# Four graph-attention layers on one core: the next batches' nodes loaded by SP instead of GpSimd, and the input test spread over layer 3 instead of layer 2

## The chip, the cores and the metric

The kernel runs on one core of a Trainium2 chip. The time is that of one execution on the device, in microseconds. I quote medians of several executions and, for comparisons, the ratio of means with its 95% interval. All executions quoted here were in the fast state; a run's profile comes from one execution of it. The profiled execution of the kernel before took 3149.0 us, 8 us less than the median of the others, so a difference between its trace and another's comes out some us smaller than that between medians. The granted TensorE clock is given as a share of full speed.

Names of the engines in the profile: PE is TensorE's matmuls, PEld its weight loads, DVE is VectorE, ACT is ScalarE, POOL is GpSimd, SP is SyncE. L409 is a line of the kernel; later kernels are a few lines shorter or longer, so the same statement has a neighbouring number.

## The reference, cut to what matters

Sixteen graphs of 1024 nodes with 256 features pass four layers of graph attention, each behind a layer norm:

```
# layer 0 (layers 1 and 2 alike with another activation; layer 3 has 4 heads)
h = maximum(layernorm(x), 0)
x = x + attention(h, adj)          # softmax over masked scores, then scores @ (h @ W)
```

`adj` is int32, 16 x 1024 x 1024. The fast path of the kernel is right only if its entries are 0 or 1, so the kernel also tests that, and falls back to a slow general path if the test fails.

## The kernel before

Two streams of batches, the even and the odd ones, run side by side, half a batch apart; a generator yields estimated times and decides whose code is traced next. The build then orders each engine's instructions itself: it may draw an instruction forward into an earlier gap, unless `keep_in_program_order` pins it behind the last instruction traced on the same engine. An engine takes its list in order, as the trace below shows for VectorE: from 455.2 us it stands idle for 2.22 us at reductions whose nodes have not landed, though the matmuls that feed the `inv` behind them end at 456.0 us.

```python
nodes = tile_pool("nodes", bufs=3)          # x_b: three buffers; adjs: four
...
def fetch_nodes(b):
    xs[b] = nodes.tile([P, NI, D], F32, name="x_b")
    queue = nc.gpsimd if b > 1 else nc.sync
    fetch = queue.dma_start(xs[b]..., in_blocks(x[b]))        # 1 MB
    if b > 0:
        tc.keep_in_program_order(fetch)

def load(b):                     # traced by batch b-2, step by step
    for c in range(4):
        ... nc.gpsimd.dma_start(rows[c], adj[b, ...])         # int32 to bytes, to DRAM; pinned
    if b < 2:
        fetch_nodes(b)
    yield
    mask = masks[b] = nodes.tile(..., name="mask")
    for c in range(4):
        ... nc.sync.dma_start_transpose(mask[:, c], ...)      # the turning transfers; pinned
        yield
    if b > 1:
        fetch_nodes(b)
        yield

def test(b):
    for i in range(NI):          # 8
        adj_i = adjs.tile([P, N], BF, name="adj_i")
        fetch = nc.gpsimd.dma_start(adj_i, adj[b, rows i])    # pinned for batch 0 only
        square = nc.scalar.activation(adj_i, adj_i, AF.Square, ..., accum_out=squares[...])
        tc.keep_in_program_order(square)
        yield
...
def first(pair):                 # a batch begins: sums for the layer norm
    nc.vector.tensor_reduce(sums[:, pair], xb[:, pair, :], AX.X, ALU.add)
    yield from project(...)
...
# finishing of a layer, row block by row block
finish(i, acc, sums[:, i : i + 1])
if l == 2:
    next(testing)
...
# layer 3: eight pieces (four heads, two halves)
for n in range(H * NH):
    ... 8 matmuls into accT
    nc.scalar.copy(sums, accT)
    next(coming, None)           # one step of load(b + 2)
    ... TensorE turns sums; inv; y; per head: bias, relu, norm, rescale
```

Of the kernel before, what the change touches and what calls it, by code (L numbers as in the profile page):

```python
# [59 lines left out]
def short_path(ctx: ExitStack, tc: tile.TileContext, ins: dict, out: bass.AP, bad: bass.AP):  # L60

    nc = tc.nc
    x, adj = ins["x"], ins["adj"]
# [31 lines left out]
    def in_blocks(a: bass.AP) -> bass.AP:  # L95
        return a.rearrange("(c p t) f -> p c t f", p=P, t=2)

    xs, masks = {}, {}
    narrows = [dram.tile([N, N // 2], BF, name=f"narrow{n}") for n in range(2)]

    def fetch_nodes(b: int):
        xs[b] = nodes.tile([P, NI, D], F32, name="x_b")
        queue = nc.gpsimd if b > 1 else nc.sync
        fetch = queue.dma_start(xs[b].rearrange("p (c t) f -> p c t f", t=2), in_blocks(x[b]))
        if b > 0:
            tc.keep_in_program_order(fetch)

# [25 lines left out]
    def test(b: int):  # L133

        for i in range(NI):

            adj_i = adjs.tile([P, N], BF, name="adj_i")
            fetch = nc.gpsimd.dma_start(adj_i, adj[b, ts(i, P), :])  # L138
            if b == 0:
                tc.keep_in_program_order(fetch)  # L140


            square = nc.scalar.activation(  # L143
                adj_i, adj_i, AF.Square, bias=minus_half, accum_out=squares[:, b, i : i + 1]
            )
            tc.keep_in_program_order(square)
            yield
# [116 lines left out]
    def accumulator(b: int) -> bass.AP:  # L264
        return psum.tile([P, HALF], F32, name=f"acc{b % 2}")
# [40 lines left out]
    def weigh(b: int, column, c, op, into: list):  # L306


        while row_taken:
            yield 0.25  # L310
        row_taken.append(b)
        r = psum.tile([P, N], F32, name="row", bufs=1)
        for i in range(NI):
            nc.tensor.transpose(r[:, ts(i, P)], column(i).to_broadcast([P, P]), ident)  # L314
        yield 0.5
        for j in range(NI):
            w = edges.tile([P, N], F32, name=f"weights{b % 2}")
            nc.vector.scalar_tensor_tensor(w, r, c(j), masks[b][:, j // 2, :, j % 2], op0=op, op1=ALU.mult)  # L318
            into.append(w)
            if j == NI - 1:  # L320
                row_taken.pop()
            yield 0.5

    def start(behind, b: int):

        for t in behind:
            if row_taken == [b]:
                return
            yield t
# [19 lines left out]
    def batch(b: int):  # L349
# [4 lines left out]
        testing = test(b)  # L354

        def begin(l: int):

            V = nodes.tile([P, NI, H, E + 1], F32, name="V", bufs=4).rearrange("p i h e -> p i (h e)")

            def evict(i: int, projected: bass.AP, rstd: bass.AP):  # L360
                nc.scalar.activation(V[:, i, D : D + 3], projected[:, D:], AF.Exp, scale=rstd)  # L361
                if l == 2:
                    nc.scalar.mul(V[:, i, :D], projected[:, :D], rstd)
                else:
                    nc.vector.tensor_scalar(  # L365
                        V[:, i, :D], projected[:, :D], rstd, V[:, i, D : D + 1],
                        op0=ALU.mult, op1=ALU.mult,
                    )

            return V, evict  # L370
# [4 lines left out]
        def begin3():  # L375
            h3 = last["h3"] = single.tile([P, NI, D], F32, name="h3")
            V3 = nodes.tile([P, NI, H, E + 1], F32, name="V", bufs=4)
            ex = last["ex"] = small.tile([P, NI, 3 * H], F32, name="ex", bufs=2)

            def evict3(i: int, projected: bass.AP, rstd: bass.AP):  # L380
                nc.scalar.activation(ex[:, i, :], projected[:, D:], AF.Exp, scale=rstd)
                nc.scalar.mul(h3[:, i, :], projected[:, :D], rstd)
                q = ex[:, i, :H].unsqueeze(2)
                nc.gpsimd.tensor_mul(
                    V3[:, i, :, :E], h3[:, i, :].rearrange("p (h e) -> p h e", h=H),
                    q.to_broadcast([P, H, E]),
                )
                nc.gpsimd.tensor_copy(V3[:, i, :, E:], q)
                nc.gpsimd.tensor_add(xb[:, i, :], xb[:, i, :], beta)

            return V3, evict3

        def attend(l: int, V: bass.AP, finish, then: int):

            weights = []
            behind = weigh(
                b, lambda i: V[:, i, D + 2 : D + 3], lambda j: V[:, j, D + 1 : D + 2],
                ALU.min if l == 1 else ALU.max, weights,
            )
            yield from start(behind, b)  # L400
            following = begin(then) if then < 3 else begin3()
            steps = iter(())
            accs = {}
            sums = small.tile([P, NI], F32, name="sums_of_x")

            def product(i: int, j: int):
                if j == 0:
                    accs[i] = accumulator(b)[:, : D + 1]
                nc.tensor.matmul(  # L409
                    accs[i], weights[j][:, ts(i, P)], V[:, j, : D + 1],  # L410
                    start=(j == 0), stop=(j == NI - 1),
                )


            for j in range(NI):
                next(behind)
                product(0, j)
                product(1, j)
                if b == 0 and j == NI - 1:


                    next(preparing)
                    if l == 0:
                        next(loading[1])
                    next(preparing, None)
                yield 0.9
            for _ in behind:
                pass
            for i in range(NI):
                if i > 1:  # L430
                    for j in range(NI):
                        product(i, j)
                acc = accs.pop(i)
                finish(i, acc, sums[:, i : i + 1])
                if l == 2:
                    next(testing)
                if i != 0:
                    yield 3.6
                if i % 2 == 1:

                    yield from steps
                    steps = project(b, then, xb, sums, i // 2, following[1])
                yield from islice(steps, 1)
            yield 1.0
            yield from steps
            return following[0]
# [9 lines left out]
        def finish(i: int, acc: bass.AP, total: bass.AP):  # L456
            add_elu(xb[:, i, :], acc, total)
# [50 lines left out]
        def weigh3(h: int):  # L508
            if h == H:
                return iter(())  # L510
            return weigh(
                b, lambda i: ex[:, i, 2 * H + h : 2 * H + h + 1],
                lambda j: ex[:, j, H + h : H + h + 1], ALU.max, weights,
            )
# [3 lines left out]
        for n in range(H * NH):  # L518
            h, g = divmod(n, NH)
            if g == NH - 1:  # L520

                behind = weigh3(h + 1)
                yield from start(behind, b)

            accT = accumulator(b)[: E + 1, :]
            for j in range(NI):
                if n == 0:
                    next(behind)
                nc.tensor.matmul(  # L529
                    accT, V3[:, j, h, :], weights[h * NI + j][:, ts(g, HALF)],  # L530
                    start=(j == 0), stop=(j == NI - 1),
                )
                if n > 0:
                    next(behind, None)
                yield 0.9
            for _ in behind:
                pass
            sums = wide.tile([E + 1, HALF], F32, name="sums")
            nc.scalar.copy(sums, accT)
            next(coming, None)  # L540
            yield 0.5
            acc = psum.tile([P, NG, E + 1], F32, name="misc")
            for i in range(NG):
                nc.tensor.transpose(acc[:, i, :], sums[:, ts(i, P)], ident[: E + 1, : E + 1])  # L544
            inv = small.tile([P, NG], F32, name="inv4")
            inverse(inv, acc[:, :, E])
            nc.vector.tensor_mul(  # L547
                y[:, ts(g, NG), h, :], acc[:, :, :E], inv.unsqueeze(2).to_broadcast([P, NG, E])
            )
            yield 0.5  # L550
            if g == NH - 1:
                if h > 0:
                    rescale(*normed.pop())
                normed.append(center(h))
                yield 1.0
# [21 lines left out]
    while streams:  # L577
        ahead = min(streams, key=lambda s: s[0])
        t = next(ahead[1], None)
# [381 lines left out]
```

## Time and profile before

| | before |
|---|---|
| time, median | 3157.41 us (3155.65 to 3158.07) |
| span of the profiled execution | 3147.4 us |
| TensorE busy | 2992.1 us, 95% |
| VectorE, ScalarE, GpSimd busy | 67%, 35%, 31% |
| node loads on GpSimd | 14, of 1 MB, 5.6 us from issue to landing |
| VectorE idle until nodes land | 68.6 us, 15 times; 6.0 us of it at the program's first load, which SP issues |

The prediction below shows the lines and reads them. TensorE's busy share looks full, but a stall can cost twice here: idle time, and a slower clock just after it (in the stretch 450 to 470 us below, 16.09 of 20 us busy and a mean clock of 0.91).

### The profile page before, as it was taken

The numbers are of one execution on the slowest core, as the hardware profiler recorded it, in microseconds if no ns is written. First come the engines' busy times: TensorE is split into PE (matmuls) and PEld (weight loads), VectorE is DVE, ScalarE is ACT, GpSimd is POOL, SyncE is SP. The second block draws the span as 40 slices with busy tenths as digits, with TensorE's granted clock in tenths as the row PEclk, the third lists the DMA queues.
The fourth block names the chain that finished last, engine by engine and source line by source line (L and its number), as shares of the span: only waits on it lengthen the run. The fifth ranks groups of instructions, "written<-read, shape, count | busy, mean of one in ns | idle before, by whom it ended". The sixth has DMA issues, their size and how long they took to land.

```text
span 3147.4 us, 36526 instructions
## 1 busy us (share of the span) xinstructions
PE 2992.1 (95%) x12678; PEld 2054.9 (65%) x12678; DVE 2122.3 (67%) x4595; ACT 1095.7 (35%) x3009; POOL 966.2 (31%) x1469
## 2 busy tenths in 40 slices
PE   7999999999999999999999999999999999999986
PEld 6776756657576675766757667575665757657652
DVE  5666677665867667676676776667766676766755
ACT  2433424234242342524324243342423424234240
POOL 2222323233242332323233232332322324233233
PEclk9999999999999999999999999999999999999998
DMA  7212212112122112212122120221211212002010
GB/s 122 37 23 38 41 27 44 18 34 41 27 47 21 41 27 41 38 17 51 18 41 41 16 52 14 41 41 27 44 18 33 41 27 48 7 14 41 1 27 15
DMA packets 116880, 105.59 MB, mean 34 GB/s; under 512 B 73680, under 2 KB 91216, under 8 KB 116688
## 3 DMA queue, kind: packets, MB, share of 16 engines
q0 software_dynamic: 44256, 81.80, 16.1%
q1 hardware_dynamic: 72432, 21.37, 3.4%
q8 instruction: 103, 1.69, 0.2%
q14 instruction: 89, 0.73, 0.1%
HBM read 153.49 MB, written 33.55 MB: 59 GB/s over the span
## 4 chain that ended last, share of the span: by engine, by line
PE 67%; DVE 20%; POOL 4%; ACT 3%; DMA 3%; issue 2%; SPq 0%; DVEq 0%; ACTq 0%; POOLq 0%
PE acc L409 32%; PE acc L529 19%; PE acc L297 11%; DVE weights L318 10%; PE misc L290 2%; DMA x_b<-in_x_dram 2%; PE row L314 2%; POOL rstd L261 2%; POOL y L489 1%; DVE x_b L345 1%; DVE x_b L344 1%; DVE sums_of_x L463 1%; DVE V L365 1%; DVE centered L274 1%; PE misc L544 1%
## 5 line engine op out<-in xcount | busy, mean ns | idle before, releaser
L409 PE MATMUL acc<-V,weights 128*128 128x257 f32 x6144 | 1446.0, 383 | 43.4 <-DVE weights L318 32.6
L409 PEld LDWEIGHTS acc<-V,weights 128*128 128x128 f32 x6144 | 1145.0, 190 | 362.4 <-DVE weights L318 107.4
L529 PE MATMUL acc<-weights,V 128*65 128x512 f32 x2048 | 965.6, 597 | 1.9 <-DVE weights L318 1.5
L318 DVE SCALAR_TENSOR_TENSOR weights<-row,ex,mask 128x1024 f32<-128x1024 f32 x512 | 630.2, 1275 | 19.6 <-PE row L314 10.6
L297 PE MATMUL acc<-W,hT 128*128 128x259 f32 (+1 forms) x2048 | 516.7, 390 | 28.3 <-ACT hT L292 12.6
L529 PEld LDWEIGHTS acc<-weights,V 128*65 128x65 f32 x2048 | 275.3, 139 | 362.5 <-issue 317.6
L318 DVE SCALAR_TENSOR_TENSOR weights<-row,V,mask 128x1024 f32<-128x1024 f32 x384 | 478.7, 1276 | 45.9 <-PE row L314 45.9
L297 PEld LDWEIGHTS acc<-W,hT 128*128 128x128 f32 x2048 | 377.7, 191 | 145.1 <-ACT hT L292 39.2
L341 ACT ACTIVATE below<-acc,inv 128x256 f32<-128x256 f32 x256 | 121.2, 473 | 751.2 <-DVE inv L334 610.2
L281 ACT ACTIVATE square<-x_b,minus_mean 128x256 bf16<-128x256 f32 x512 | 260.4, 509 | 306.5 <-DVE minus_mean L271 297.8
L261 POOL TENSOR_TENSOR rstd<-rstd,minus_half 128x2 f32<-128x2 f32 (+1 forms) x320 | 298.1, 932 | 21.1
L489 POOL TENSOR_TENSOR y<-y,bias 128x512 f32<-128x512 f32 x64 | 81.7, 1276 | 668.1 <-DVE y L547 637.9
L260 POOL TENSOR_SCALAR rstd<-squared 128x2 f32<-128x2 f32 x256 | 64.7, 253 | 639.7 <-ACT square L281 639.0
L292 ACT ACTIVATE hT<-misc 128x512 f32<-128x512 f32 x256 | 149.6, 597 | 211.7 <-PE misc L290 210.3
L274 DVE TENSOR_SCALAR centered<-x_b,minus_mean 128x256 f32<-128x256 f32 x512 | 167.0, 371 | 52.8 <-PE misc L290 48.9
L344 DVE SCALAR_TENSOR_TENSOR x_b<-below,x_b 128x256 f32<-128x256 f32 x256 | 123.0, 481 | 100.4 <-ACT below L341 99.9
L290 PEld LDWEIGHTS misc<-ident,centered 128*128 128x128 f32 x1024 | 126.6, 143 | 88.4 <-issue 50.8
L361 ACT ACTIVATE V<-acc,rstd 128x3 f32<-128x3 f32 x384 | 97.8, 260 | 242.0 <-PE acc L297 241.3
L138 POOL DMA_DIRECT2D adj_i<-in_adj_dram x128 | 76.6, 599 | 338.9 <-ACT adj_i L143 185.5
L333 DVE TENSOR_SCALAR inv<-acc 128x1 f32<-128x1 f32 x256 | 38.6, 154 | 209.6 <-PE acc L409 208.2
L290 PE MATMUL misc<-ident,centered 128*128 128x128 f32 x1024 | 155.8, 278 | 19.0 <-DVE centered L274 18.8
L365 DVE TENSOR_SCALAR V<-acc,rstd,V 128x256 f32<-128x256 f32 x256 | 133.9, 539 | 57.6 <-ACT V L361 56.8
(74 smaller groups left out, 2165.3 us busy)
## 6 DMA issues: line engine op xcount, KB each, us to landing
adj_i<-in_adj_dram POOLq DMA_DIRECT2D x128, 256.0 KB, 3.9
narrow<-in_adj_dram POOLq DMA_DIRECT2D x64, 256.0 KB, 9.4
out_dram<-y POOLq DMA_DIRECT2D x32, 512.0 KB, 4.0
x_b<-in_x_dram POOLq DMA_DIRECT2D x14, 1024.0 KB, 5.6
x_b<-in_x_dram SPq DMA_DIRECT2D x2, 1024.0 KB, 7.4
mask<-narrow SPq DMA_TRANSPOSE x64, 3.7
W<-in_L_gnn_W_dram SPq DMA_DIRECT2D x3, 256.0 KB, 6.4
weights<-in_L_gnn_a_dram SPq DMA_DIRECT2D x3, 256.0 KB, 8.1
```

The lines of the kernel that those rows point to most:

```text
L261: nc.gpsimd.tensor_tensor(r, r, minus_half.to_broadcast([P, n]), op=ALU.pow)
L274: nc.vector.tensor_scalar(centered[:, n, :], xb[:, 2 * pair + n, :], minus_mean[:, n : n + 1], 0.0, op0=ALU.add, op1=ALU.max,)
L281: nc.scalar.activation(square, xb[:, 2 * pair + n, :], AF.Square, bias=minus_mean[:, n : n + 1], accum_out=squared[:, n : n + 1],)
L290: nc.tensor.transpose(turned[:, k, ts(n, P)], centered[:, n, ts(k, P)], ident)
L292: nc.scalar.mul(hT, turned, ROOT_D)
L297: nc.tensor.matmul(projected, hT[:, k, ts(n, P)], W[l][:, k, :], start=(k == 0), stop=(k == NK - 1),)
L318: nc.vector.scalar_tensor_tensor(w, r, c(j), masks[b][:, j // 2, :, j % 2], op0=op, op1=ALU.mult)
L341: nc.scalar.activation(below, acc[:, :D], AF.Exp, scale=inv)
L344: nc.vector.scalar_tensor_tensor(xi, below, 1.0, xi, op0=ALU.min, op1=ALU.add)
L365: nc.vector.tensor_scalar(V[:, i, :D], projected[:, :D], rstd, V[:, i, D : D + 1], op0=ALU.mult, op1=ALU.mult,)
L409: nc.tensor.matmul(accs[i], weights[j][:, ts(i, P)], V[:, j, : D + 1], start=(j == 0), stop=(j == NI - 1),)
L529: nc.tensor.matmul(accT, V3[:, j, h, :], weights[h * NI + j][:, ts(g, HALF)], start=(j == 0), stop=(j == NI - 1),)
```

## The change

The intent: take the loads of later nodes out of GpSimd's busy list and put them on SP, behind the turning transfers of the same batch; and take the test's row loads and squares out of layer 2, where ScalarE has an elu per row, into the eight pieces of layer 3. The whole diff:

```diff
@@ fetch_nodes
-        queue = nc.gpsimd if b > 1 else nc.sync
-        fetch = queue.dma_start(xs[b]..., in_blocks(x[b]))
+        fetch = nc.sync.dma_start(xs[b]..., in_blocks(x[b]))
@@ finishing of a layer
                 finish(i, acc, sums[:, i : i + 1])
-                if l == 2:
-                    next(testing)
@@ layer 3, each piece
             nc.scalar.copy(sums, accT)
+            next(testing)
             next(coming, None)
```

More of the change, by code (lines that the diff above doesn't have):

```diff
@@ L102, in fetch_nodes @@
         xs[b] = nodes.tile([P, NI, D], F32, name="x_b")
-        queue = nc.gpsimd if b > 1 else nc.sync
-        fetch = queue.dma_start(xs[b].rearrange("p (c t) f -> p c t f", t=2), in_blocks(x[b]))
+        fetch = nc.sync.dma_start(xs[b].rearrange("p (c t) f -> p c t f", t=2), in_blocks(x[b]))
         if b > 0:
```

## The prediction

> **What bounds the kernel now.** I began with the page: busy shares first, then the chain that ended last.
>
> ```profile
> span 3147.4 us, 36526 instructions
> PE 2992.1 (95%) x12678; PEld 2054.9 (65%) x12678; DVE 2122.3 (67%) x4595; ACT 1095.7 (35%) x3009; POOL 966.2 (31%) x1469
> ...
> PE 67%; DVE 20%; POOL 4%; ACT 3%; DMA 3%; issue 2%; SPq 0%; DVEq 0%; ACTq 0%; POOLq 0%
> PE acc L409 32%; PE acc L529 19%; PE acc L297 11%; DVE weights L318 10%; PE misc L290 2%; DMA x_b<-in_x_dram 2%; PE row L314 2%; POOL rstd L261 2%; POOL y L489 1%; DVE x_b L345 1%; DVE x_b L344 1%; DVE sums_of_x L463 1%; DVE V L365 1%; DVE centered L274 1%; PE misc L544 1%
> ```
>
> TensorE is the bound: 95% busy, 155 us of the span idle. About 12 us of that is the start (its first wait is 12.1 us) and some 40 us are the last 150 us, where one stream is left (108 busy of 150). So about 100 us of idle is spread over the steady part. The odd line is a transfer, the nodes of a later batch, with 2% of the chain, though it is needed only when the next batch begins. I therefore asked who TensorE waits for, and who waits for the nodes.
>
> ```profile
> engine line waited for: us in total, times, longest us
> PE misc L544 <- ACT sums L539: 35.1, 19, 4.9
> PE acc L409 <- DVE weights L318: 32.6, 42, 1.7
> PE misc L290 <- DVE centered L274: 18.8, 8, 12.1
> ```
>
> The longest class is TensorE waiting for ScalarE's copy of the layer-3 sums, up to 4.9 us a time. The timeline around one node load shows where it comes from (start, duration, then in brackets the idle time before it and who ended it):
>
> ```profile
> 451.55 0.86 POOL L104 DMA_DIRECT2D x_b<-in_x_dram  x1
> ...
> 454.52 0.69 DVE L502 TENSOR_TENSOR y<-y,rstd 128x512 f32<-128x512 f32 x1 [2.80 <-POOL rstd L261]
> ...
> 457.43 2.46 DVE L463 TENSOR_REDUCE sums_of_x<-x_b 128x2 f32<-128x512 f32 x4 [2.22 <-DMA x_b<-in_x_dram]
> 459.81 0.15 DVE L333 TENSOR_SCALAR inv<-acc 128x1 f32<-128x1 f32 x1
> ...
> 461.60 0.46 PE L544 MATMUL misc<-ident,sums 65*128 65x65 f32 x4 [3.90 <-ACT sums L539]
> ```
>
> VectorE stands at the reductions of the next batch's nodes, which the build has drawn forward into a gap: this stream's present batch ends its layer 3 only at 521 us. VectorE works in order, so `inv` behind them comes late, ScalarE's `below` and then its sums copy come late, and TensorE loses 3.90 us. GpSimd issued the load at 451.55 because the load is pinned behind GpSimd's other work in the middle of layer 3; it landed 5.8 us later. Then the price, in busy time by stretch of 20 us (length, then PE, PEld, DVE, ACT, POOL, then the granted TensorE clock, DMA share, GB/s):
>
> ```profile
> 430.00:450.00 20.00, 20.00 (x81) 12.42 (x80) 17.96 (x42) 6.24 (x17) 5.22 (x6) 1.00 0.53 50
> 450.00:470.00 20.00, 16.09 (x62) 10.09 (x61) 9.83 (x19) 3.93 (x11) 6.20 (x7) 0.91 0.16 53
> 470.00:490.00 20.00, 20.00 (x75) 11.65 (x73) 13.51 (x31) 6.75 (x17) 6.96 (x7) 1.00 0.29 54
> ...
> 510.00:530.00 20.00, 16.89 (x83) 13.60 (x81) 16.54 (x36) 10.85 (x29) 9.76 (x13) 1.00 0.33 79
> ...
> 650.00:670.00 20.00, 18.94 (x82) 12.22 (x81) 13.34 (x25) 3.78 (x10) 2.55 (x3) 1.00 0.17 54
> ```
>
> The stretch with the load lacks 3.9 us of TensorE time, and its mean clock is 0.91, some 1.4 us more on 16.1 us of work: 5.3 us. The next load (issued at 650.41, landed at 656.0, VectorE idle 7.58 us for it) costs only 1.1 us, because TensorE had other queued work. The two kinds alternate with the parity of the batch, every 386 us for the pair.
>
> **What the Trainium skill says.** "DMA: Bandwidth & Descriptors", section "Issuing engines are not separate DMA queues", says that the issuing engine changes only who spends issue time: all transfers run on the same 16 engines. The trace agrees: an issue of nodes took 0.86 us on GpSimd and 0.44 on SP, and the landings took 5.6 and 7.4 us, the two on SP in the crowded start. So the move cannot make the transfer faster; only its time of issue can matter. The same page's "Rules for kernel authors" advises issuing early and waiting late, which is the point of this change. "SBUF — State Buffer", section "SBUF: two separate sides", says VectorE and GpSimd share a port pair that one of them holds for a whole instruction. The trace fits: a VectorE add of 0.43 us (L344) took 1.27 at 520.43 us, beside a GpSimd add of 520.14 to 521.42. "Perfetto Trace Analysis", section "Identifying the Most-Contended Engine", warns that matmul busy time is no measure of distance to the limit. It holds here: four L529 matmuls that normally start 0.43 us apart were shown as 3.02 us busy after that stall.
>
> **The change, part by part.**
>
> *Nodes by SP.* Removed: 14 issues of 0.86 us on GpSimd, 12 us in 3147 on an engine 31% busy; worth almost nothing. Moved: the load of batch b now waits for its batch's four turning transfers and for the buffer of batch b-3 (three buffers), no longer for GpSimd's place in layer 3 of b-2.
>
> ```profile
> 477.99 5.25 SPq L124 DMA_TRANSPOSE mask<-narrow  x4
> ...
> 520.14 1.28 POOL L504 TENSOR_TENSOR y<-y,x_b 128x512 f32<-128x512 f32 x1
> ```
>
> These turns are batch 4's and end at 483.2 us; the last reader of batch 1's nodes is GpSimd's add that ends at 521.4. So batch 4's load leaves SP at about 521.5 instead of 650.4, and lands at about 528 (estimate from landings of 5.6 to 7.4 us). It comes some 130 us earlier, long before its batch begins. Batch 2 finds a fresh buffer and loads near 88 us instead of 263. If VectorE never stands at a load again, the gain is 7 loads of one parity by 5.3 us, 37 us, plus six of the other parity by 1.1 us, 7 us (the first load, at 263, cost TensorE nothing): 44 us, 1.4%.
>
> *The test.* Eight row loads (0.59 us each on GpSimd) and eight squares (1.15 + 0.20 us on ScalarE) per batch go from layer 2's finishing into the eight pieces of layer 3. No work is removed: 16 x 8 x 1.35 = 173 us of ScalarE, an engine 35% busy. In layer 2 two squares at 520.65 and 522.50 us push back the elu of the last layer-1 and layer-2 rows by about 1 us each, and soon after TensorE waits 1.08 us for `centered` (526.46). GpSimd also stood 185.5 us in all at row loads waiting for earlier squares; in layer 3 the pieces are some 16 us apart (130 us over 8), so those waits should shrink. A square sits behind the sums copy, so it does not delay TensorE's next transposes but may delay the other stream's elu or hT by up to 1.35 us. I count a gain of 0.5 us a batch, 8 us, and a cost of the same order: net +0 to 10 us gained.
>
> **The rivals.**
>
> 1. *The stall moves.* The reductions (2.46 us) are drawn forward to where the build believes the nodes have landed, and it has been too hopeful by 2 to 7.6 us at all 14 GpSimd loads (68.6 us of VectorE waiting in total). The new place is right after batch b-3's last add, in layer 2's finishing of the other stream, where every row needs `inv` and two adds of VectorE in turn. For: the misjudgement does not depend on the queue. Against: much of VectorE's work is queued there and may be put ahead. A return of half the loss costs 20 us of the 44; a full return with the worse parity on every load, 14 x 5.3 = 74 us lost instead of 44, would give 3187.
> 2. *More gain than the stall.* With nodes there 130 us earlier, more of the next batch's layer 0 can fill gaps. The stretch 510 to 530, where batches change, lacks 3.1 us; such gaps come at each change of batch, so 14 x 3 = 42 us is the reserve. A quarter of it is 10 us. It would take both full gains to reach 2%.
> 3. *The squares hurt layer 3.* VectorE's `y` waits for GpSimd's `y L489` there; a row load standing in front of it by 2 us in every piece, half of it reaching TensorE, would cost 128 x 1 = 128 us in the worst case. The row loads' squares will have been done long before, so I give this little weight.
> 4. *Nothing*, if the lost stretches were filled by waits behind them: about 3155.
>
> **Range and chances.** 44 us times a bit over half surviving rival 1 is 25, plus 3 net for the test and the gaps: 28 us. 3157 - 28 = 3129 us. A full success of everything gives about 3095; a moved stall about 3160. I take 3098 to 3162 for 8 in 10. Faster by over 2% means under 3094.3, which needs the whole stall gone and a good part of rival 2: 0.1. Slower by over 2% means over 3220.6, needing rival 3: 0.02. Within 2%: 0.88.
>
> **What would show it.** Right: node loads on SP at about 325, 521 and 710 us, just behind the last adds of b-3; VectorE's wait for the nodes falls from 68.6 us to under 20; TensorE's wait for the sums copy falls from 35.1 to about 10; the stretches at mid layer 3 show full TensorE and a clock of 1.00. Rival 1: the wait for the nodes stays at 30 us or more and TensorE lacks time just after 325, 521, 710. Rival 3: longer waits of GpSimd at the row loads and of VectorE for `y`. I would be wrong outright if the loads on SP landed later than now, or if the changed order of VectorE's stream cost more than the stall.

## The result, and the profile after

The changed kernel took 3116.24 us (3115.17 to 3116.99, four executions), the kernel before 3157.74 us beside it. The ratio is 0.9867, 95% interval 0.985 to 0.9884. A ratio here is the mean time of one kernel's fast runs over that of the other's in the same rounds, so it is not quite the ratio of the two medians. The kernel gained 1.3%: inside the predicted range, on the side of "within 2%", and 13 us better than the predicted time.

The page of the changed kernel, head and chain of work that ended last:

```profile
span 3114.5 us, 36472 instructions
PE 2991.3 (96%) x12678; PEld 2054.2 (66%) x12678; DVE 2113.3 (68%) x4595; ACT 1112.7 (36%) x3009; POOL 961.1 (31%) x1455
...
PE 76%; DVE 15%; ACT 3%; POOL 3%; issue 3%; DMA 1%; SPq 0%; DVEq 0%; ACTq 0%; POOLq 0%
```

TensorE's share of the chain rose from 67 to 76%, and the transfers' fell from 3 to 1%. Its busy time is unchanged (2992.1 and 2991.3 us), so in sum what went is its idle time (e5 below shows what hides behind the sum). Whom TensorE waited for, in the changed kernel:

```profile
engine line waited for: us in total, times, longest us
PE acc L408 <- DVE weights L317: 32.5, 41, 1.7
PE misc L289 <- DVE centered L273: 17.3, 16, 12.0
...
PE misc L542 <- ACT sums L536: 5.7, 12, 0.7
```

The wait for the sums copy fell from 35.1 to 5.7 us, and its longest from 4.9 to 0.7 us; the other two classes stayed nearly as they were. VectorE's wait for the nodes, first in the kernel before and then in the changed one, where only the very first load of the program is left:

```profile
DVE sums_of_x L463 <- DMA x_b<-in_x_dram: 68.6, 15, 7.7
```

```profile
DVE sums_of_x L460 <- DMA x_b<-in_x_dram: 5.9, 1, 5.9
```

The stretches of the prediction, in the changed kernel (same columns):

```profile
450.00:470.00 20.00, 19.88 (x80) 12.14 (x79) 14.27 (x34) 6.75 (x17) 7.27 (x9) 1.00 0.19 27
...
510.00:530.00 20.00, 17.67 (x86) 14.15 (x85) 15.34 (x38) 8.25 (x23) 9.47 (x12) 1.00 0.34 105
650.00:670.00 20.00, 20.00 (x88) 13.33 (x87) 14.55 (x29) 6.27 (x17) 6.10 (x8) 1.00 0.27 34
```

The stretch at 450 us has 19.88 us of TensorE for 16.09 and a clock of 1.00 for 0.91; the stretch at 650 has 20.00 for 18.94. The change of batch, 510 to 530, still lacks 2.3 us.

The load of batch 4's nodes left SP where the prediction put it, at 521 us (the timeline of SP):

```profile
521.35 0.37 SPq L103 DMA_DIRECT2D x_b<-in_x_dram  x1
```

What I had wrong is where the reductions went. The timeline of VectorE in the changed kernel, reductions for batch 3, whose nodes had landed at 336 us:

```profile
450.15 0.68 DVE L460 TENSOR_REDUCE sums_of_x<-x_b 128x2 f32<-128x512 f32 x1
...
450.87 0.68 DVE L460 TENSOR_REDUCE sums_of_x<-x_b 128x2 f32<-128x512 f32 x1
...
451.86 0.68 DVE L460 TENSOR_REDUCE sums_of_x<-x_b 128x2 f32<-128x512 f32 x1
...
455.22 0.68 DVE L460 TENSOR_REDUCE sums_of_x<-x_b 128x2 f32<-128x512 f32 x1
```

They stay in the middle of layer 3, at practically the old place (VectorE had reached them at 455 us before), now spread one by one into small gaps, and wait for nothing. The stall did not move with the load.

Two side effects are visible. The node loads now land 6.5 us after issue, and the output stores, which leave GpSimd at the same moment (both follow the batch's last add), take 7.6 us for 4.0; nobody waits for either. And GpSimd stood 628.9 us in total at row loads whose buffer an earlier square still held, for 185.5 us before: the squares are pinned to the pieces, while the build draws the row loads forward.

### The profile page after: what moved, and what is told of

Its sections match the earlier page's. It is cut to its first block, busy times and chain, and to the rows that moved or that the text cites. A ratio compares the mean times of both kernels' runs of the same rounds, so it can differ in the third digit from the quotient of the medians.

```text
span 3114.5 us, 36472 instructions
## 1 busy us (share of the span) xinstructions
PE 2991.3 (96%) x12678; PEld 2054.2 (66%) x12678; DVE 2113.3 (68%) x4595; ACT 1112.7 (36%) x3009; POOL 961.1 (31%) x1455
## 3 DMA queue, kind: packets, MB, share of 16 engines
q8 instruction: 103, 1.69, 0.2%
## 4 chain that ended last, share of the span: by engine, by line
PE 76%; DVE 15%; ACT 3%; POOL 3%; issue 3%; DMA 1%; SPq 0%; DVEq 0%; ACTq 0%; POOLq 0%
PE acc L408 36%; PE acc L526 22%; PE acc L296 12%; DVE weights L317 8%; PE misc L289 3%; PE row L313 2%; ACT square L280 1%; PE misc L542 1%; POOL y L486 1%; DVE V L364 1%; DVE x_b L344 1%; POOL rstd L260 1%; DVE x_b L343 1%; ACT below L340 1%; DVE y L487 1%
## 5 line engine op out<-in xcount | busy, mean ns | idle before, releaser
L526 PE MATMUL acc<-weights,V 128*65 128x512 f32 x2048 | 955.3, 592 | 1.9 <-DVE weights L317 1.5
L137 POOL DMA_DIRECT2D adj_i<-in_adj_dram x128 | 77.6, 606 | 640.6 <-ACT adj_i L142 628.9
L536 ACT COPY sums<-acc 65x512 f32<-65x512 f32 x128 | 74.1, 579 | 247.2 <-PE acc L526 247.2
```

The lines of the kernel that those rows point to most:

```text
L526: nc.tensor.matmul(accT, V3[:, j, h, :], weights[h * NI + j][:, ts(g, HALF)], start=(j == 0), stop=(j == NI - 1),)
```

## The experiments

Theory A: the gain is the time at which the nodes are issued. VectorE stood at reductions drawn forward to where the build thought the nodes landed, and TensorE paid; whoever issues the load early enough takes that away. Theory B: the gain, or a good part of it, is the test's move out of layer 2. A second rival to A: it is not the time but the issuing engine, GpSimd, whose list and descriptor work delays the load.

### e1: the nodes alone on SP

```diff
-        queue = nc.gpsimd if b > 1 else nc.sync
-        fetch = queue.dma_start(...)
+        fetch = nc.sync.dma_start(...)
```

> Only the node loads go to SP; the test stays in layer 2. In the built program TensorE's order is the same as before, and VectorE's differs only in where the four reductions of the next nodes stand. Theory A (the gain is the wait of VectorE at the nodes): 3112 to 3125 us, VectorE's wait for the nodes under 10 us, TensorE's wait for the sums copy under 10 us. Theory B (the gain is the test's move out of layer 2's crowded ScalarE): 3145 to 3160 us.

3109.02 us, ratio 0.9846 (0.983 to 0.9862), under theory A's 3112 even. VectorE waited 5.8 us for nodes and TensorE 8.3 us for the sums copy. Since TensorE's list is the same as before, instruction by instruction, one can ask of each matmul how much earlier it starts. From the start times in the two traces:

| matmul number | start before, us | earlier in e1 by, us |
|---|---|---|
| 1600 | 393 | -2.1 |
| 2000 | 502 | 3.4 |
| 2400 | 591 | 3.4 |
| 2800 | 694 | 4.7 |
| 3200 | 783 | 4.7 |
| 3600 | 891 | 11.5 |
| 12000 | 2925 | 42.5 |

The gain comes in steps, and each step is at a node load: 5.5 us at 451, 1.3 at 650, 6.8 at 838. Between loads almost nothing is gained. Over all 14 loads the steps are 3.5 to 6.8 us for the odd batches, 1.3 to 1.5 us for the even ones, and none at the first, at 263 us. That is the prediction's alternation of 5.3 and 1.1 us, seen directly.

### e2: the test alone in layer 3

```diff
-                if l == 2:
-                    next(testing)
...
             nc.scalar.copy(sums, accT)
+            next(testing)
             next(coming, None)
```

> Only the test moves to layer 3; the nodes stay on GpSimd in mid layer 3. Theory A: 3145 to 3165 us, VectorE's wait for the nodes stays near 60 us or grows, since GpSimd's row loads now stand ahead of the node load. Theory B: 3112 to 3130 us.

This was a miss: 3109.43 us, ratio 0.9849 (0.9832 to 0.9865), as good as e1. Theory B seemed to win, until GpSimd's timeline told something else:

```profile
405.73 0.65 POOL L138 DMA_DIRECT2D adj_i<-in_adj_dram  x1 [13.65 <-ACT adj_i L143]
406.38 0.77 POOL L104 DMA_DIRECT2D x_b<-in_x_dram  x1
```

The node load is issued at 406 us, not at 451. In each piece the test's row load is traced just ahead of the node load, so the pin ties the node load to a row load, and row loads are free to be drawn forward. The node load went forward with it. So e2 had changed the time of issue too, by accident, and could not tell A from B. e6 repairs that.

### e3: the nodes on GpSimd, four pieces earlier

```diff
+        if b > 1:
+            fetch_nodes(b)
         mask = masks[b] = nodes.tile(..., name="mask")
         for c in range(NI // 2):
             ...
-        if b > 1:
-            fetch_nodes(b)
-            yield
```

> The nodes stay on GpSimd, but are issued at the first piece of layer 3, four pieces (some 50 us) earlier than before; VectorE, TensorE and ScalarE have the same order as in the run with the nodes alone on SP. Theory A in the form 'the time of issue, not the issuing engine': 3112 to 3128 us, wait for the nodes under 10 us. Rival (GpSimd's descriptor work or its queue is the cost): 3145 us or more.

3106.9 us, ratio 0.9841 (0.9824 to 0.9857). The load left GpSimd at 386.8 us for 451.5, still on GpSimd, and the whole gain is there. SP is not needed for it.

### e4: the nodes on SP, as late as before

```diff
+        fetch = nc.sync.dma_start(...)
+        # wait for the GpSimd instruction that stood before the load
+        tc.add_manual_dep(fetch.ins, last_on_gpsimd.name, Sync, ...)
```

> The nodes on SP, but held until the GpSimd instruction that stood before the load in the kernel before has finished; VectorE, TensorE and ScalarE have exactly the order of the kernel before. Time of issue: 3148 to 3165 us, VectorE's wait for the nodes near 70 us again or somewhat more (SP landings took 6.5 us against 5.7). Rival (the engine matters): 3112 to 3130 us.

3150.62 us, ratio 0.998 (0.9964 to 0.9997). The timeline:

```profile
451.23 0.38 SPq L103 DMA_DIRECT2D x_b<-in_x_dram  x1
...
453.46 0.69 DVE L510 TENSOR_TENSOR y<-y,rstd 128x512 f32<-128x512 f32 x1 [2.12 <-POOL rstd L269]
...
457.15 1.28 DVE L471 TENSOR_REDUCE sums_of_x<-x_b 128x2 f32<-128x512 f32 x2 [3.00 <-DMA x_b<-in_x_dram]
```

It is the picture of before with another engine's name on it. VectorE waited 69.7 us for nodes in all (68.6 before). Issued at the same place, the load took 5.3 us to land from SP (median) and 5.6 us from GpSimd, and the issue itself 0.37 and 0.86 us. e3 and e4 together settle the rival: early on GpSimd gives everything, late on SP gives nearly nothing.

### e5: the changed kernel again

No edit; it ran on one chip with e6 to e8.

> The changed kernel, unaltered, on the chip of these runs. Both halves together gave 3116 us on another chip, where each half alone gave 3109 here. If that difference is the chip: 3107 to 3112 us. If the halves hinder each other: 3113 to 3119 us.

3116.68 us, ratio 0.9881 (0.9865 to 0.9898), with the kernel before at 3154.78 us, within 1 us of its 3155.65 beside e1 to e4. So the second reading holds: the halves hinder each other, and both together are some 7 us slower than either alone. By matmul number (the order of TensorE's list differs from e1's in 3% of the places, and in 1 to 6% in the comparisons below) e5 is 2.8 us behind e1 at about 395 us and still only 3.4 us at 2886, so most of it falls in the first layer 3 and in the end. For the first layer 3 the timeline of the changed kernel shows why:

```profile
247.18 1.15 ACT L142 ACTIVATE adj_i<-adj_i,minus_half 128x1024 bf16<-128x1024 bf16 x1 [13.60 <-DMA adj_i<-in_adj_dram]
```

ScalarE stands 13.6 us at a pinned square. Batch 0's row loads are pinned, and this one is issued right behind four byte-making loads of `adj`; it landed 11.9 us later, for the usual 3.9. ScalarE's elu comes late, and TensorE waits 2.50 us for it at 249.20 (2.74 us in e5).

The other part, some 3 us between 2963 and 3058 us, is a slower clock in the traces: e5 runs at half of full speed for 6.83 us from 2979.4 us and for 3.41 us from 3020.4 us, where e1 runs at full speed. Up to the last matmul e5 has 27.3 us at half speed and e1 13.7. TensorE's idle time before matmuls is in sum no longer in e5 (98.0 us for 100.3), its busy time is (2991.3 us for 2981.6). So a good part of the 7 us is matmuls at a slower clock. The pause of 1.7 us before the first of these stretches is in e1 too (2976 us), and there no half speed follows it; what decides it is not shown.

### e6: the test in layer 3, its step behind the load's step

```diff
             nc.scalar.copy(sums, accT)
-            next(testing)
             next(coming, None)
+            next(testing)
```

(Beside e2: two lines change places. The nodes are on GpSimd.)

> The test in layer 3 and the nodes on GpSimd, as in the run with the test alone, but in each piece the test's step comes after the load's step, so the node load is pinned behind the bias add and the inverse root again and no longer behind a row load that the build draws forward. Time of issue alone: 3148 to 3162 us, VectorE's wait for the nodes over 50 us, node loads issued near 450 and 650 us. Rival (moving the test out of layer 2 is worth something by itself): 3110 to 3140 us.

3162.57 us, ratio 1.0023 (1.0006 to 1.004). The node loads left at 456.4 and 654.9 us, VectorE waited 70.0 us for nodes, and the gain is gone. So the test's move by itself is worth nothing; it costs about 7 us beside the kernel before (2 to 13 by the interval). e2's whole gain was the accident of the pin. Theory B falls.

### e7: the nodes late, the reductions pinned to the start of the batch

```diff
-            nc.vector.tensor_reduce(sums[:, pair], xb[:, pair, :], AX.X, ALU.add)
+            tc.keep_in_program_order(
+                nc.vector.tensor_reduce(sums[:, pair], xb[:, pair, :], AX.X, ALU.add)
+            )
```

> The kernel before, nodes late on GpSimd, but the four reductions of the next nodes are pinned to their place at the start of the batch and can't be drawn forward into layer 3. If the stall is VectorE standing at the reductions: its wait for the nodes falls under 10 us, though the load is as late as before, and the time is 3105 to 3130 us. Rival (the drawn-forward reductions are needed at the change of batch): the nodes cause no wait, but TensorE lacks as much at the change of batch, and the time is 3145 us or more.

3208.98 us, ratio 1.0176 (1.0159 to 1.0193): slower, as the rival said, and by more. First the kernel before, at two changes of batch, then e7 in mid layer 3 and at the same changes of batch:

```profile
500.00:550.00 50.00, 46.10 (x224) 37.50 (x223) 38.76 (x80) 22.59 (x61) 18.28 (x28) 1.00 0.24 48
700.00:750.00 50.00, 47.70 (x224) 38.86 (x224) 33.85 (x84) 24.83 (x66) 21.66 (x36) 1.00 0.27 53
```

```profile
450.00:470.00 20.00, 20.00 (x78) 12.47 (x77) 14.71 (x32) 6.70 (x19) 6.47 (x9) 1.00 0.33 58
500.00:550.00 50.00, 43.30 (x183) 30.17 (x182) 31.07 (x72) 24.00 (x70) 18.48 (x27) 0.93 0.17 38
...
700.00:750.00 50.00, 42.56 (x178) 30.46 (x177) 31.79 (x68) 21.66 (x60) 17.52 (x27) 0.90 0.18 38
```

The stall is gone: full TensorE at 450 to 470 us with nodes that landed at 471 us, later than in any other run. So it was the reductions that VectorE stood at. But the change of batch lacks 7 us of TensorE for 2 to 4 before, with a lower clock, because the next batch's layer 0 can't begin ahead: TensorE's wait for `centered` rose from 18.8 to 41.6 us, and for the weights from 32.6 to 65.8. The drawn-forward reductions are needed; what was wrong was only that their data came late.

### e8: no test at all

```diff
+    nc.vector.memset(squares, 0.0)
...
-            next(testing)
```

The guard against other inputs is gone on purpose; the outputs are right on these inputs.

> The changed kernel without the test at all: no row loads, no squares, the flag's tile set to zero (the outputs stay right on these inputs, the guard against other inputs is gone, on purpose). If GpSimd's 629 us at the row loads and the squares cost nothing on the path: 3108 to 3117 us, within 8 us of the changed kernel on this chip. If the test in layer 3 costs: 3085 to 3105 us.

3097.27 us beside e5's 3116.68 on the same chip: the test costs 19 us in the changed kernel. By matmul number the difference is 2.9 us at 398 us of e5 and 13.0 at 2886, so after the start it grows by about 0.8 us a batch. Beside e1, which has the test in layer 2, e8 is 12 us faster, on another chip; so most of the test's cost was there before the change. The third rival's path is not where it lies: VectorE's wait for GpSimd's `y` is 49.8 us in e5 and 49.2 without the test. Whether it is GpSimd's waits at the row loads or ScalarE's squares I can't say: four more row buffers, which would have told them apart, do not fit into the memory (the build refused them).

### e9, e10 and e11: from the fastest kernel on

e11 is e3 unaltered; e9 is e3 with the test in layer 0's finishing; e10 is e3 with layer 0's scaling of the values taken from VectorE:

```diff
# e9
-                if l == 2:
+                if l == 0:
                     next(testing)
# e10
+                elif l == 0:
+                    scale = small.tile([P, 1], F32, name="scale0")
+                    nc.gpsimd.tensor_mul(scale, V[:, i, D : D + 1], rstd)
+                    nc.scalar.mul(V[:, i, :D], projected[:, :D], scale)
```

> The fastest so far (nodes on GpSimd at the first piece of layer 3, 3106.9 us) with the test moved to layer 0's finishing, where ScalarE has no elu. The run without any test was 19 us faster than the changed kernel, so there is something to win by its place: if the squares cost by standing before the elu of the same stream, 3095 to 3104 us. Rival (a square costs wherever it stands, or hurts the start, where batch 0's layer 0 runs with little else): 3106 to 3118 us.

> The same fastest kernel, with layer 0's scaling of the values (eight VectorE instructions of 0.54 us a batch) given to ScalarE, behind a small product on GpSimd. The stretch where batches change lacks some 5 us of TensorE each time and waits there for VectorE's weights. If VectorE's load is what binds there: 3085 to 3102 us. Rival (the longer way over GpSimd and ScalarE holds the accumulators): 3110 to 3140 us.

> The nodes on GpSimd at the first piece of layer 3, unaltered, beside the two above on one chip: 3105 to 3110 us.

e11 took 3106.47 us, ratio 0.9858 (0.9841 to 0.9874), which confirms e3. e9 took 3111.8 us, slower. By matmul number it is 13.4 us behind e11 at 215 us and only 7.9 us at 2887: it loses at the start, where batch 0's layer 0 stands alone (TensorE waits 10.0 us once there for ScalarE's values, behind a square whose row load took 12.6 us to land), and then wins 0.4 us a batch. A test in layer 0 from batch 1 on would be the next thing to try.

e10 took 3086.22 us, ratio 0.9798 (0.9781 to 0.9814): 20 us faster than e11 on the same chip and 30 us faster than the changed kernel. TensorE's wait for VectorE's weights fell from 32.6 us in e11 to 18.6, and for `centered` from 18.0 to 11.8; but its wait for ScalarE's `above` rose from 5.0 to 20.1. Its idle time before matmuls fell by only 7.2 us in sum (97.9 to 90.7), its busy time by 14.1, of which some 3.4 fit the shorter time at half clock (10.2 us for 17.1; half the difference, an estimate). The gain by matmul number grows evenly, 1.5 us at 393 us and 20.3 at 2859. So VectorE's load does bind; that it binds at the changes of batch alone is not shown. This version beats both kernels clear of noise, though whether it is over 2% faster than the kernel before stays unclear by its interval.

### e12: the same for layer 1 too

```diff
-                elif l == 0:
+                else:
```

> The last run's step carried to layer 1 as well: its scaling of the values too goes from VectorE to ScalarE behind a small GpSimd product. In layer 1 TensorE hardly waits, and ScalarE has an elu per row in the finishing that follows, so I expect little: 3080 to 3090 us beside 3086 us with layer 0 alone. If ScalarE's elu is pushed back: 3092 us or more.

3098.07 us, ratio 0.9826 (0.981 to 0.9843): a miss on the bad side, 12 us worse than e10 (whose kernel ran on another chip; the kernel before was 3153.09 and 3152.38 us beside them). TensorE's wait for the sums copy rose from 7.8 to 10.0 us, which fits ScalarE being pushed back, but is too little to be the whole cause. I leave it open.

## Why the prediction was right, point by point

- *The bound and the stall.* Right. TensorE's idle behind the sums copy came from VectorE standing at the nodes; e7 shows that the reductions were the place, e3 and e4 that the time of the load's issue decided.
- *Its price, 44 us.* Right in mechanism and size. e1 moves TensorE's work forward in steps of 3.5 to 6.8 and 1.3 to 1.5 us at the loads (predicted 5.3 and 1.1), 44.6 us between 393 and 2925 us. Both parts of the price are seen: from the kernel before to e1 TensorE's idle time before matmuls fell by 32.0 us, its busy time by 10.5. One reading was off: the 68.6 us are not all at the 14 GpSimd loads, 6.0 are the first load's, so 62.6. And the 3.02 us of the four matmuls after the stall are a slower clock: half of full speed from 462.5 to 465.9 us.
- *Where the loads would go.* Right: 521.35 us for "about 521.5", and 329.90 for "about 325", as batch 0 ended somewhat later.
- *The first rival, "the stall moves".* Wrong, and this is the step that failed: "The new place is right after batch b-3's last add". The reductions stayed in mid layer 3, over 110 us behind the landing of the nodes. I had taken the old place to be the place of the believed landing, and it hardly depends on the landing: batch 3's nodes land at 457 us in the kernel before, 393 in e3, 336 in the changed kernel and 332 in e1, and VectorE comes to their reductions at 455, 446, 450 and 447 us. What in the build's ordering holds them there is not shown. So the weight of "a bit over half surviving", 25 of 44 us, was the term mis-sized. The full 44 us were there.
- *The test, "net +0 to 10 us gained", counted as 3.* Wrong in sign. e6 is about 7 us slower than the kernel before, e2 2.5 us slower than e3, and e8 shows that the test in layer 3 costs 19 us in all. The pinned rows of batch 0, behind four other transfers, were not in my sum. Nor did the waits of GpSimd "shrink": they grew from 185.5 to 628.9 us. I had spaced the row loads with the pieces, but only the squares are held there.
- *"Removed: 14 issues of 0.86 us on GpSimd ... worth almost nothing."* Right: e1 beside e3, same lists on the other engines, is not faster. SP even loses some 3 us at the very end (last section).
- *The second rival, more gain than the stall.* Not seen: 510 to 530 us went from 16.89 to 17.67 us of TensorE. e10 shows that the reserve there was real, and that VectorE's load was its key.
- *The third rival.* The waits of GpSimd at the row loads grew as it feared, but they did not reach VectorE: its wait for GpSimd's `y` was 49.9 us for 55.9 before.

In sum: 3157.7 less about 48 for the nodes (ratio 0.9846 of e1), plus some 7 for the test's new place, is 3117; measured 3116. I predicted 28 us of gain from 25 and 3; it was 48 and minus 7. That the number came as near as 13 us is in part luck: 23 us too little for the nodes and 10 too much for the test have opposite signs.

## What to carry to other kernels

When an engine that works in order waits for data of a later stage, ask first when the load was issued and what its issue was pinned to: here moving it earlier, on either engine, was worth 1.5%, and moving it to another engine at the same time nearly nothing. When two edits come together, run each alone and look at what else it changed; e2 gained everything by an accident of the order in which two steps were traced, and only swapping two lines showed it. A busy share of 95% hides stalls that a table of start times, instruction by instruction, shows as steps.

## What the Trainium skill lacked or had wrong

- "TensorE: Matmul & The Clock Gate", section "Part 1: The HAM clock gate", says that the array falls to half its clock after an idle window of about 3.4 us. The runs agree in part. In the kernel before, six of the seven stalls of 3.58 to 4.86 us at the odd batches' loads went with half the clock for 3.41 or 6.83 us, and cost 5.2 to 6.8 us matmul by matmul; the seventh, of 3.64 us, did not and cost 3.5. But a pause of only 1.68 us (1.69 in the changed kernel) at a change of batch was followed by it too, once in 8 before and 4 times in 8 in the changed kernel. Single pauses of 1.1 us were not.
- "DMA: Bandwidth & Descriptors", section "Anatomy of one DMA — SWDGE (gpsimd) path", gives 2.0 us + bytes / 436 GB/s, which is 4.4 us for 1 MB (an estimate from that page). The node loads from GpSimd took 5.6 us from issue to landing at the median. The table in the section "Bandwidth" of the same page gives 6.15 us for 1 MB on the DMA engines alone, which is more than the whole landing took here.
- No page tells of a last drain of GpSimd as long as here. It took 6.3 to 6.4 us in the kernels with the nodes on SP and the test kept (changed kernel, e1, e4) and 3.0 to 3.3 us in those with the nodes on GpSimd, so the former end some 3 us later. Without the test (e8, nodes on SP) it took 3.6 us, so the number of GpSimd's transfers alone does not explain it; the cause is open.
